# x + beta by accumulating DMA in every fourth group of a conditional residual adapter

## The chip, the cores and the metric

The kernel runs on one core of one Trainium2 chip. The metric is device time in microseconds, the median of the runs; the profile comes from one further execution. Engine names are those of the profile: PE is TensorE (PEld its weight loads), DVE is VectorE, ACT is ScalarE, POOL is GpSimd, SP is SyncE. A "q" behind an engine's name is its queue of instructions that aren't counted as work, DMA issues among them.

## The reference

There are 128 batches of 128 rows by 512 columns in float32, and 10 sets of weights. Batch b uses the set that `itok[b]` names.

```python
def ref(x, ids, W1, b1, W2, b2, gamma, beta):      # x: (128, 128, 512)
    h = relu(einsum('bsh,bha->bsa', x, W1[ids]) + b1[ids])      # A = 128
    z = x + einsum('bsa,bah->bsh', h, W2[ids]) + b2[ids]
    n = (z - mean(z)) * rsqrt(var(z) + 1e-5)
    return x + n * gamma[ids] + beta[ids]
```

## The kernel before

A batch is one tile of 128 rows by 512 columns. x is loaded in groups of four batches (1024 KB each) into four buffers by `load_x`, and the result is stored in pairs of batches (512 KB) by `store`; both are issued on SP. All ten rows of beta, gamma and b2 are first spread over the 128 partitions (`beta_b`, `gamma_b`, `b2_b`), and all of W1 and W2 stay in SBUF.

For one batch the work is this. PE transposes x in four pieces (`transpose_x`, L218), ACT copies the transpose out of PSUM (L222) and stages the batch's W1 (L209). PE multiplies (`down`, L241, 8 instructions), ACT applies the ReLU (L249), PE multiplies with W2 into a PSUM tile `py` (`up`, L258, 2 instructions), of which there are five. DVE adds the residual and sums the row (`residual`, L273), ACT sums squares (`square`, L288). DVE multiplies with gamma (`scale`, L322) and, once the reciprocal deviation of the pair is there (L305 to L317), multiplies and adds `o` in place (`finish`, L331). SP stores the pair.

The bias b2 enters in one of three ways. By default POOL makes r = x + b2 (`add_b2`, L228; four buffers), and the residual adds r in place of x. In some batches PE adds b2 by a small bfloat16 matmul ahead of the main one in `up` (`b2_by_matmul`, L257, 22 batches). In 13 others DVE adds it (`b2_by_vector`, L271). POOL also makes o = x + beta for every batch (`add_beta`, L235), into tiles of two batches, of which there are five.

The main loop is software-pipelined. Its iteration b has POOL make r of batch b + 2 and o of batch b; PE does `transpose_x` of b + 3, `down` of b + 2 and `up` of b + 1; DVE does the residual of b, `scale` of b - 2 and `finish` of b - 3. The store of a pair follows its second `finish`, in even iterations: iteration b stores the pair of batches b - 4 and b - 3. `keep` chains every instruction of an engine to the one before it, so that each engine's order is the order in which the program is written. In the kernel before, the stores are the exception: they are left to the scheduler.

For the last four batches the loop hands over to `tail`. There ACT normalizes batches 123, 124 and 125, and POOL multiplies two of them with gamma and adds o for all three (`by_pool`, L384 and L386, five instructions), while DVE finishes the rest. SP stores batches 122 to 127 one by one, in order (`store_last`, L389).

The first 16 batches use an early copy of W1 in another layout (`w1e`); the four loads of the later copy (`load_w1`, L111) are spread over the first iterations of the loop. A register that holds the batch's set number is loaded for four batches at a time on each engine that needs it (`lid`, L188).

Of the kernel before, what the change touches and what calls it, by code (L numbers as in the profile page):

```python
# [8 lines left out]
FP = mybir.dt.float32  # L9
# [3 lines left out]
ALU = mybir.AluOpType  # L13
ET = mybir.EngineType
PSUM = bass.MemoryType.PSUM

P = 128
G = 4
# [6 lines left out]
def cond_resid_kernel(ctx: ExitStack, tc: tile.TileContext, x, itok, W1, b1, W2, b2, gamma, beta, out):  # L25
# [8 lines left out]
    nc = tc.nc  # L34
    B, S, H = x.shape
    L, _, A = W1.shape
    KC = H // P
    NG = B // G
# [5 lines left out]
    def keep(ins):  # L44

        engine = ins.ins.engine
        if engine in last:
            tc.add_manual_dep(ins.ins, last[engine], behind, reason="kept order")
        last[engine] = ins.ins.name
        return ins  # L50
# [1 line left out]
    const = ctx.enter_context(tc.tile_pool(name="const", bufs=1))  # L52
    xp = ctx.enter_context(tc.tile_pool(name="xp", bufs=4))
    rp = ctx.enter_context(tc.tile_pool(name="rp", bufs=4))
    op = ctx.enter_context(tc.tile_pool(name="op", bufs=5))
    tp = ctx.enter_context(tc.tile_pool(name="tp", bufs=2))
    wp = ctx.enter_context(tc.tile_pool(name="wp", bufs=3))
    st = ctx.enter_context(tc.tile_pool(name="st", bufs=6))
# [5 lines left out]
    xs = {}  # L64

    def load_x(g):
        t = xp.tile([P, G, H], FP, tag="x", name=f"x_{g}")
        keep(nc.sync.dma_start(out=t, in_=x[g * G : (g + 1) * G].rearrange("b s h -> s b h")))
        xs[g] = t

    def xb(b):
        return xs[b // G][:, b % G, :]
# [27 lines left out]
    for l in range(0, L, 5):  # L100
        keep(
            nc.sync.dma_start(
                out=w1e[:, l : l + 5].rearrange("p l k a -> p l (k a)"),
                in_=W1[l : l + 5].rearrange("l (p k) a -> p l (k a)", k=KC),
# [4 lines left out]
    def load_w1(k):  # L109
        keep(  # L110
            nc.sync.dma_start(out=w1[:, :, k, :], in_=W1[:, k * P : (k + 1) * P, :].rearrange("l p a -> p l a"))  # L111
        )

    for l in range(0, L, 5):
        keep(
            nc.sync.dma_start(
                out=w2[:, l * H : (l + 5) * H].rearrange("p (l h) -> p l h", l=5),
                in_=W2[l : l + 5].rearrange("l a h -> a l h"),
# [48 lines left out]
    beta_b = const.tile([P, L * H], FP, name="beta_b")  # L167
# [14 lines left out]
    lids, xT, w1s, hT, rs, os, ys, ssqs, nmeans, rstds = {}, {}, {}, {}, {}, {}, {}, {}, {}, {}  # L182
    phs, pxs, sums = {}, {}, {}

    def lid(b, engine):
        g = b // G
        if (g, engine) not in lids:
            loads, vals = nc.values_load_multi_w_load_instructions(  # L188
                lang[0:1, g * G : (g + 1) * G],
                engines=[engine],  # L190
                min_val=0,
                max_val=L - 1,
                skip_runtime_bounds_check_because="clamped on the chip to 0..L-1 above",
            )
            for ins in loads:
                keep(ins)
            lids[g, engine] = vals
        return lids[g, engine][b % G]

    def b2_by_matmul(b):  # L200
        return b < 4 or (b % 4 == 1 and not b2_by_vector(b))

    def b2_by_vector(b):
        return b % 8 == 5 and 8 <= b < B - 16

    def stage_w1(b):
        w1s[b] = wp.tile([P, KC, A], FP, tag="w1s", name=f"w1s_{b}")
        src = (w1e if b < EARLY else w1).rearrange("p l k a -> p (l k a)")[:, bass.ds(lid(b, ET.Activation) * (KC * A), KC * A)]
        keep(nc.scalar.copy(w1s[b].rearrange("p k a -> p (k a)"), src))  # L209

    def transpose_x(b):
        pxs[b] = p_x.tile([P, KC, P], FP, tag="xT", name=f"pxT_{b}")
        for k in range(KC):
            if b < EARLY:
                cols = xb(b).rearrange("s (p k) -> s k p", k=KC)[:, k, :]
            else:
                cols = xb(b)[:, k * P : (k + 1) * P]
            keep(nc.tensor.transpose(pxs[b][:, k, :], cols, ident))  # L218

    def copy_xT(b):  # L220
        xT[b] = tp.tile([P, KC, P], FP, tag="xT", name=f"xT_{b}")
        keep(nc.scalar.copy(xT[b], pxs.pop(b)))  # L222

    def add_b2(b):
        if not b2_by_matmul(b) and not b2_by_vector(b):
            rs[b] = rp.tile([P, H], FP, tag="r", name=f"r_{b}")
            v = lid(b, ET.Pool)
            keep(nc.gpsimd.tensor_tensor(rs[b], xb(b), b2_b[:, bass.ds(v * H, H)], ALU.add))  # L228

    def add_beta(b):  # L230
        g, j = divmod(b, 2)
        if j == 0:
            os[g] = op.tile([P, 2, H], FP, tag="o", name=f"o_{g}")
        v = lid(b, ET.Pool)
        keep(nc.gpsimd.tensor_tensor(os[g][:, j, :], xb(b), beta_b[:, bass.ds(v * H, H)], ALU.add))  # L235

    def down(b):
        phs[b] = p_h.tile([P, P], FP, tag="h", name=f"ph_{b}")
        for k in range(KC):
            keep(  # L240
                nc.tensor.matmul(  # L241
                    phs[b], lhsT=w1s[b][:, k, :], rhs=xT[b][:, k, :], start=(k == 0), stop=(k == KC - 1)
                )
            )
        del xT[b], w1s[b]

    def relu(b):
        hT[b] = tp.tile([P, P], FP, tag="hT", name=f"hT_{b}", bufs=6)
        keep(nc.scalar.activation(hT[b], phs.pop(b), AF.Relu, bias=b1T[:, bass.ds(lid(b, ET.Activation), 1)]))  # L249

    def up(b):
        v = lid(b, ET.PE)
        ys[b] = p_y.tile([P, H], FP, tag="y", name=f"py_{b}")
        m = b2_by_matmul(b)
        if m:
            pick_b = pick[:, bass.ds(v + 2 * L, 1)].to_broadcast([96, P])
            keep(nc.tensor.matmul(ys[b], lhsT=pick_b, rhs=parts[:96, :], start=True, stop=False))  # L257
        keep(nc.tensor.matmul(ys[b], lhsT=hT[b], rhs=w2[:, bass.ds(v * H, H)], start=not m, stop=True))  # L258
        del hT[b]
# [5 lines left out]
    def residual(b):  # L265
        r = rs.pop(b) if b in rs else xb(b)
        if b % 2 == 0:
            sums[b // 2] = st.tile([P, 2], FP, tag="sum", name=f"sum_{b // 2}")
        if b2_by_vector(b):
            v = lid(b, ET.DVE)  # L270
            keep(nc.vector.tensor_tensor(ys[b], ys[b], b2_b[:, bass.ds(v * H, H)], ALU.add))  # L271
        keep(
            nc.vector.scalar_tensor_tensor(ys[b], ys[b], 1.0, r, ALU.mult, ALU.add, accum_out=col(sums, b))  # L273
        )
# [57 lines left out]
        )  # L332

    def store(g):
        nc.sync.dma_start(out=out[2 * g : 2 * g + 2].rearrange("b s h -> s b h"), in_=os.pop(g))
        del rstds[g]

    def on(b):
        return 0 <= b < B
# [151 lines left out]

    for i in range(3, B + U):
        b = i - U - 1
        if b > 0 and b % G == 0 and b // G + 3 < NG:
            load_x(b // G + 3)
        if i == 5:
            load_x(3)
        if i in (4, 6, 8, 10):
            load_w1((i - 4) // 2)
        if i == 4:  # L500
            up(2)
        if i == 5:
            up(3)
        if i > 3 and on(i):
            transpose_x(i)
        if b <= E:
            add_b2(b + 2)
            add_beta(b)
        if i > 4 and on(i - 1):
            down(i - 1)  # L510
        if i > 3 and on(i):
            copy_xT(i)
        if i > 4 and on(i + 1):
            stage_w1(i + 1)
        if i > 4 and on(i - 1):
            relu(i - 1)
        if i > 5 and on(i - U):
            up(i - U)


        g, half = divmod(b, 2)
        p = g - 1
        mine, old = 0 <= p < B // 2, 0 <= p - 1 < B // 2
        if b == E:
            add_b2(b + 3)
            add_beta(b + 1)
            add_b2(b + 4)
            for n in range(b + 2, B):
                add_beta(n)
        if b > E:  # L530
            tail(b)
        elif half == 0:
            if on(b):
                residual(b)
            if mine:
                rstd_1(p)
                scale(2 * p)
            if on(b):
                negative_mean(b)
            if mine:  # L540
                rstd_2(p)
            if old:
                finish(2 * p - 1)
                store(p - 1)
            if mine:
                rstd_3(p)
        else:
            if on(b):
                residual(b)
            if mine:  # L550
                rstd_4(p)
                scale(2 * p + 1)
            if on(b):
                negative_mean(b)
            if mine:
                finish(2 * p)
        if 0 <= b <= E:
            square(b)
            if half == 1:
                deviation(g)  # L560

        for n, engine in ((i + 3, ET.Activation), (i - U + 3, ET.PE), (b + 1, ET.DVE), (b + 5, ET.Pool)):
            if on(n):
                lid(n, engine)
# [37 lines left out]
```

## Time and profile before

| | us |
|---|---|
| median of 3 runs | 313.74 (313.61 to 314.29) |
| profiled execution | 313.83 |
| its span, first to last instruction | 312.1 |
| POOL, o = x + beta (L235), 128 of them | 161.6 busy, 1274 ns each |
| POOL, r = x + b2 (L228), 93 of them | 118.5 busy, 1274 ns each |
| PE, b2 by matmul (L257), 22 of them | 8.4 busy, 381 ns each |
| DVE, b2 (L271), 13 of them | 9.0 busy, 692 ns each |
| DMA, over the span | 75.49 MB, mean 242 GB/s |

In a row of groups, the busy time is the union of the instructions' times; an instruction's own duration can overlap its neighbours, so the distance from one start to the next is often shorter than the duration. "Idle before" is the time in which the engine stood still just ahead of such an instruction, with what ended it. The mean TensorE clock granted was 0.99. DMA issues list the time from issue to landing: 5.8 us at the median for a group of x, 3.9 for the store of a pair.

### The profile page before, as it was taken

Reading aid. Unit: us, or ns where it says so; the run is one execution under the profiler, and the core shown is the slowest. Engines: PE = TensorE matmul, PEld = TensorE weight load, DVE = VectorE, ACT = ScalarE, POOL = GpSimd, SP = SyncE. Lnnn points to the kernel's source line nnn. Section 1 sums busy time; section 2 is a strip of 40 time slices with the busy share of each in tenths; the row PEclk is TensorE's granted clock in tenths of the full one; section 3 lists DMA queues with packets and bytes.
Section 4 is the critical chain, followed back from the end, with each engine's and each line's share of the span. In section 5 each row is a group of like instructions: output and inputs, shape, how many; then the busy total and the mean of one; then the engine's idle time right before and its main releaser. Section 6 shows DMA issues by size and latency. Waiting matters only on the chain.

```text
span 312.1 us, 7096 instructions
## 1 busy us (share of the span) xinstructions
PE 300.5 (96%) x1869; PEld 223.8 (72%) x1869; DVE 297.3 (95%) x945; ACT 285.4 (91%) x724; POOL 280.1 (90%) x234
## 2 busy tenths in 40 slices
PE   8999999999999999999999999999999999999970
PEld 3567787777777767777777777777777777777740
DVE  6677999999999999999999999999999999999995
ACT  3878999999999999999999999999999999999982
POOL 1319978999999999999999999999999999999963
PEclk9999999999999999999999999999999999999995
DMA  6999998767776777667666567576666667633234
GB/s 209 387 387 352 326 339 275 238 229 226 236 250 225 255 265 269 242 231 270 257 227 226 210 238 253 213 272 269 232 232 198 232 247 239 244 134 138 88 149 168
DMA packets 42313, 75.49 MB, mean 242 GB/s; under 512 B 1785, under 2 KB 6916, under 8 KB 42274
## 3 DMA queue, kind: packets, MB, share of 16 engines
q1 hardware_dynamic: 42214, 75.00, 68.6%
q8 instruction: 15, 0.25, 0.3%
q14 instruction: 24, 0.20, 0.2%
q10 hardware_dynamic: 60, 0.05, 0.1%
HBM read 41.49 MB, written 33.55 MB: 240 GB/s over the span
## 4 chain that ended last, share of the span: by engine, by line
PE 91%; DVE 5%; ACT 1%; issue 1%; DVEq 1%; DMA 1%; ACTq 0%
PE ph L241 36%; PE py L258 34%; PE pxT L218 18%; PE py L257 1%; PE row L175 1%; DVE py L273 1%; DVE gamma_b L180 1%; DVE py L322 1%; DVE o L331 1%; DMA rows<-in_L_cond_b_dram 1%; ACT sq L366 0%; DVEq L597 0%; ACT n L382 0%; DVE left L156 0%; DVE left L154 0%
## 5 line engine op out<-in xcount | busy, mean ns | idle before, releaser
L235 POOL TENSOR_TENSOR o<-x,beta_b 128x512 f32<-128x512 f32 x128 | 161.6, 1274 | 12.8 <-ACT beta_b L178 9.2
L241 PE MATMUL ph<-xT,w1s 128*128 128x128 f32 x1024 | 135.6, 275 | 0.5 <-ACT w1s L209 0.5
L258 PE MATMUL py<-w,hT 128*128 x256 | 131.1, 594 | 0.0
L228 POOL TENSOR_TENSOR r<-x,b_b 128x512 f32<-128x512 f32 x93 | 118.5, 1274 | 11.5 <-DMA x<-in_x_dram 9.2
L241 PEld LDWEIGHTS ph<-xT,w1s 128*128 128x128 f32 x1024 | 124.7, 192 | 2.4 <-ACT w1s L209 1.0
L218 PEld LDWEIGHTS pxT<-ident,x 128*128 128x128 f32 x512 | 65.5, 148 | 64.9 <-issue 44.8
L322 DVE SCALAR_TENSOR_TENSOR py<-py,nmean,gamma_b 128x512 f32<-128x512 f32 x126 | 93.8, 745 | 0.2 <-issue 0.2
L331 DVE SCALAR_TENSOR_TENSOR o<-py,rstd,o 128x512 f32<-128x512 f32 x122 | 91.0, 746 | 0.0
L288 ACT ACTIVATE sq<-py,sum 128x512 f32<-128x512 f32 x124 | 85.3, 688 | 1.4 <-DVE py L273 1.3
L222 ACT COPY xT<-pxT 128x512 f32<-128x512 f32 x128 | 73.8, 577 | 9.8 <-PE pxT L218 6.3
L218 PE MATMUL pxT<-ident,x 128*128 128x128 f32 x512 | 77.4, 274 | 0.0
L209 ACT COPY w1s<-w 128x512 f32 x112 | 69.5, 621 | 0.0
L273 DVE SCALAR_TENSOR_TENSOR py<-py,r 128x512 f32<-128x512 f32 x93 | 64.6, 694 | 1.3 <-PE pxT L218 0.6
L249 ACT ACTIVATE hT<-ph,b1T 128x128 f32<-128x128 f32 x128 | 47.4, 370 | 1.0 <-PE ph L241 1.0
L258 PEld LDWEIGHTS py<-w,hT 128*128 128x128 f32 x256 | 40.6, 192 | 2.4 <-ACT hT L249 0.7
L273 DVE SCALAR_TENSOR_TENSOR py<-py,x 128x512 f32<-128x512 f32 x35 | 24.4, 697 | 1.6 <-ACT sq L288 0.6
L288 ACT ACTIVATION_READ_ACCUMULATOR sq<-py,sum 128x1 f32 x124 | 25.7, 208 | 0.0
L299 ACT ACTIVATE sd<-ssq,eps 128x2 f32<-128x2 f32 x62 | 18.3, 296 | 2.1
L279 DVE TENSOR_SCALAR nmean<-sum 128x1 f32<-128x1 f32 x128 | 19.5, 152 | 0.1
L305 DVE RECIPROCAL stat<-sd 128x2 f32<-128x2 f32 x62 | 13.0, 210 | 1.0 <-ACT sd L299 1.0
L273 DVE DVE_READ_ACCUMULATOR py<-py,r 128x1 f32 x93 | 13.4, 144 | 0.0
L317 DVE RECIPROCAL rstd<-stat 128x2 f32<-128x2 f32 x62 | 10.4, 168 | 0.0
(56 smaller groups left out, 120.6 us busy)
## 6 DMA issues: line engine op xcount, KB each, us to landing
out_dram<-o SPq DMA_DIRECT2D x61, 512.0 KB, 3.9
x<-in_x_dram SPq DMA_DIRECT2D x30, 1024.0 KB, 5.8
w1e<-in_L_cond_W_dram SPq DMA_DIRECT2D x2, 1280.0 KB, 8.7
w<-in_L_cond_W_dram SPq DMA_DIRECT2D x2, 1280.0 KB
w<-in_L_cond_W_dram SPq DMA_DIRECT2D x4, 640.0 KB, 15.2
x<-in_x_dram SPq DMA_DIRECT2D x4, 512.0 KB, 8.4
out_dram<-o SPq DMA_DIRECT2D x6, 256.0 KB, 2.0
rows<-in_L_cond_beta_dram ACTq DMA_DIRECT2D x1, 20.0 KB
```

What stands on the lines that cost most here:

```text
L209: keep(nc.scalar.copy(w1s[b].rearrange("p k a -> p (k a)"), src))
L218: keep(nc.tensor.transpose(pxs[b][:, k, :], cols, ident))
L222: keep(nc.scalar.copy(xT[b], pxs.pop(b)))
L228: keep(nc.gpsimd.tensor_tensor(rs[b], xb(b), b2_b[:, bass.ds(v * H, H)], ALU.add))
L235: keep(nc.gpsimd.tensor_tensor(os[g][:, j, :], xb(b), beta_b[:, bass.ds(v * H, H)], ALU.add))
L241: nc.tensor.matmul(phs[b], lhsT=w1s[b][:, k, :], rhs=xT[b][:, k, :], start=(k == 0), stop=(k == KC - 1))
L249: keep(nc.scalar.activation(hT[b], phs.pop(b), AF.Relu, bias=b1T[:, bass.ds(lid(b, ET.Activation), 1)]))
L258: keep(nc.tensor.matmul(ys[b], lhsT=hT[b], rhs=w2[:, bass.ds(v * H, H)], start=not m, stop=True))
L273: nc.vector.scalar_tensor_tensor(ys[b], ys[b], 1.0, r, ALU.mult, ALU.add, accum_out=col(sums, b))
L288: nc.scalar.activation(sq, ys[b], AF.Square, bias=col(sums, b), scale=-float(H), accum_out=col(ssqs, b))
L322: nc.vector.scalar_tensor_tensor(ys[b], ys[b], col(nmeans, b), gamma_b[:, bass.ds(v * H, H)], ALU.add, ALU.mult)
L331: nc.vector.scalar_tensor_tensor(o, ys.pop(b), rstds[g][:, j : j + 1], o, ALU.mult, ALU.add)
```

## The change

In every fourth group q of four batches (q = 3, 7, ..., 27), o = x + beta is no longer made by POOL. SP first copies the four batches' rows of `beta_b` into a tile `od` of four batches by four DMAs from SBUF to SBUF (`fill_beta`, in iteration 4q - 5). In iteration 4q - 2 POOL issues one DMA that adds the group's x onto that tile (`add_x`). `finish` and `store` then use the two halves of the tile as the `o` of the two pairs. There is one `od` tile, and four `o` tiles in place of five.

With that, b2 by matmul stays for batches 0 to 3 alone. DVE adds b2 in one batch of 16 from batch 21 to batch 101 in place of one of 8, and POOL makes r for all the others.

Groups of x from the fourth on are loaded two iterations later than before, and stores are kept in the program's order on SP.

```diff
-    op = ctx.enter_context(tc.tile_pool(name="op", bufs=5))
+    op = ctx.enter_context(tc.tile_pool(name="op", bufs=4))
+    od = ctx.enter_context(tc.tile_pool(name="od", bufs=1))
...
     def b2_by_matmul(b):
-        return b < 4 or (b % 4 == 1 and not b2_by_vector(b))
+        return b < 4
 
     def b2_by_vector(b):
-        return b % 8 == 5 and 8 <= b < B - 16
+        return b % 16 == 5 and 8 <= b < B - 16
...
+    def beta_by_dma(q):
+
+        return q % 4 == 3 and q < NG - 2
+
+    def fill_beta(q):
+
+        o = od.tile([P, G, H], FP, tag="od", name=f"od_{q}")
+        os[2 * q], os[2 * q + 1] = o[:, 0:2, :], o[:, 2:4, :]
+        for j in range(G):
+            v = lid(q * G + j, ET.SP)
+            keep(nc.sync.dma_start(out=o[:, j, :], in_=beta_b[:, bass.ds(v * H, H)]))
+        return o
+
+    def add_x(q, o):
+        keep(nc.gpsimd.dma_start(out=o, in_=xs[q], accum_op=ALU.add))
+
     def add_beta(b):
         g, j = divmod(b, 2)
+        if beta_by_dma(b // G):
+            return
...
     def store(g):
-        nc.sync.dma_start(out=out[2 * g : 2 * g + 2].rearrange("b s h -> s b h"), in_=os.pop(g))
+        keep(nc.sync.dma_start(out=out[2 * g : 2 * g + 2].rearrange("b s h -> s b h"), in_=os.pop(g)))
...
-        if b > 0 and b % G == 0 and b // G + 3 < NG:
+        if b > G and b % G == 2 and b // G + 3 < NG:
             load_x(b // G + 3)
...
+        q, at = divmod(b + 5, G)
+        if at == 0 and beta_by_dma(q):
+            filled = fill_beta(q)
+        q, at = divmod(b + 2, G)
+        if at == 0 and beta_by_dma(q):
+            add_x(q, filled)
         if b <= E:
             add_b2(b + 2)
             add_beta(b)
```

## The prediction

> **What bounds the kernel now.** I read the table of engines first, then the chain that ended last, the chain in order of time, the waits, and last the timeline of POOL beside that of DVE.
>
> ```profile
> PE 300.5 (96%) x1869; PEld 223.8 (72%) x1869; DVE 297.3 (95%) x945; ACT 285.4 (91%) x724; POOL 280.1 (90%) x234
> ...
> PE 91%; DVE 5%; ACT 1%; issue 1%; DVEq 1%; DMA 1%; ACTq 0%
> ```
>
> Four engines are above 90%, so shares alone decide nothing; the chain puts 91% on PE. Its pieces give PE's price for one batch:
>
> ```profile
> 179.74 0.89 PE ph L241 x8
> ...
> 181.93 0.89 PE ph L241 x8
> 182.82 0.22 PE py L257
> ...
> 184.34 0.89 PE ph L241 x8
> ```
>
> A batch without the L257 matmul takes 181.93 - 179.74 = 2.19 us, one with it 184.34 - 181.93 = 2.41. So the matmul costs 0.22 on the path, not the 381 ns that its row in the groups gives one, which overlaps its neighbours. DVE runs just under PE's pace: its residuals at 251.00, 253.05 and 255.24 are 2.12 apart on average. It lies one batch behind PE.
>
> POOL is the engine to watch. A POOL row says 1274 ns, but back to back one starts every 1.234 (252.11 to 261.97 holds eight). With 6 r and 8 o in eight batches it needs 14 x 1.234 = 17.3 of PE's 17.74, so it gains and runs ahead until it has no free r buffer:
>
> ```profile
> POOL n L384 <- ACT n L382: 2.3, 1, 2.3
> POOL r L228 <- DVE stat L305: 2.2, 6, 0.4
> ```
>
> ```profile
> 252.11 1.27 POOL L228 TENSOR_TENSOR r<-x,b_b 128x512 f32<-128x512 f32 x1
> 257.29 0.69 DVE L273 SCALAR_TENSOR_TENSOR py<-py,r 128x512 f32<-128x512 f32 x1
> ```
>
> In the timelines, the first line is r of batch 108, POOL's first work of iteration 106; the second is DVE's residual of batch 106. POOL's lead is 257.29 - 252.11 = 5.2 us there. The wait for n is what remains of it at the end: POOL is done with the last o at 298.7 and waits 2.3 for n of batch 123. After that five POOL instructions run without a gap to 307.41, and DVE ends at 308.74:
>
> ```profile
> 300.98 1.27 POOL L384 TENSOR_TENSOR n<-n,gamma_b 128x512 f32<-128x512 f32 x1 [2.28 <-ACT n L382]
> 304.93 2.48 POOL L386 TENSOR_TENSOR o<-n,o 128x512 f32<-128x512 f32 x2
> 307.33 1.41 DVE L393 SCALAR_TENSOR_TENSOR o<-py,rstd,o 128x512 f32<-128x512 f32 x2
> ```
>
> SP stores batch 125 (POOL's last) ahead of 126 and 127. POOL's last instruction can be late by about 0.6 (308.74 - 307.41, less two issues of 0.33 to 0.4) before it moves the end.
>
> **The Trainium skill.** "DMA: Bandwidth & Descriptors", SWDGE vs HWDGE vs iDMA: accumulation is only for DMAs issued from GpSimd, whose cores write the descriptors. Its section Latency and other measured facts puts the first byte at about 1 us because of that emission; the kernel before issues no DMA from POOL, so nothing here confirms it. "Collectives: The Full Stack", The bandwidth ceiling: the fold count and why AG ≠ RS ≠ AR: an adding DMA reads two sources per write and moves half as fast as a copy; not shown here either. "SBUF — State Buffer", SBUF: two separate sides: DVE holds GpSimd off the shared port in two-port modes or with two SBUF inputs. The trace shows no sign of such a lock: POOL's x instructions last 1256 to 1307 ns beside a DVE that is always busy. Its matrix operations mostly read one operand from PSUM, so I charge nothing for it.
>
> **Part by part.**
>
> *PE:* L257 goes from 22 to 4 (batches 0 to 3): 18 x 0.22 = 3.96 us less on the path.
>
> *DVE:* L271 goes from 13 to 6. Seven adds of about 0.7 lie beside PE; they only widen DVE's margin and buy nothing. ACT is unchanged.
>
> *POOL:* r rises from 93 to 118, o falls from 128 to 100: 25 - 28 = -3 instructions, 3.7 us less, and seven accumulating DMAs. In 16 batches POOL needs 27 x 1.234 = 33.3 plus one descriptor generation, c, where PE now needs 16 x 2.19 = 35.04: a margin of 1.7 - c. I take c = 1.0 from the skill's price. Below, 0.5: the mean cost can hardly be under the 0.3 to 0.9 of a register load on POOL's queue. Above, 2.5 (an estimate: the 1 us plus a doubled read side and a start that overlaps nothing).
>
> *SP and DMA:* 7 register loads (0.3 to 1.2 on other queues) and 28 fills of 256 KB on SP, in program order between stores. They cost nothing while SP waits for DVE, which its own waits show for most of the span. Transfers rise by 7 MB of fills and 7 MB of adds with twice the reads, over 75.5 MB now. The engines are at 0.64 to 0.72 between 60 and 260 us, so the mean fits; bunching is a rival below. Loading x two batches later leaves 7 iterations, 15 us, to its transpose against a median landing of 5.8: no cost. Kept stores move two w1 loads behind stores that wait for DVE at 32.6 and 36.6; from their bytes I put the last at 44 to 45, and ACT first needs it at 49.15: no cost.
>
> *The new wait:* POOL's adding DMA waits for the fills to land. Behind it on POOL stand r of the next batches, which DVE waits for. The fills stand on SP behind the store of iteration 4q-6, which waits for DVE, so POOL can no longer be ahead by more than the fills allow. For q = 27, in the clock of before: that store is issued at 251.05; add 0.37 for it, 0.7 for the register load, 4 x 0.5 for the fills: 254.1. Landing takes 2.0 at best (a 256 KB store in the tail), so 256.1; by bytes, 1.57 MB at 240 GB/s give 257.6 and more. I take 256.6. POOL may start r of 108 at 256.6 + 1.0 = 257.6, not at 252.1. The lead of 5.2 is gone.
>
> *What that costs at the end:* from there to n of 123 POOL has 20 r and 18 o: 38 x 1.234 = 46.9, so 304.5. PE's clock has by then gained 14 x 0.22 = 3.08 before 106, so 301.4; five instructions of the tail take 6.43: 307.8. SP then issues three stores, the last 0.8 later, and before there were 3.3 from DVE's end to the span's end: 307.8 + 0.8 + 3.3 = 311.9. PE alone would have given 312.1 - 3.96 = 308.1. **The tail on POOL thus takes back about 3.8 of the 3.96.**
>
> *What the first group costs:* for q = 3 the fills follow the w1 load on SP, at about 40 to 42, behind 3.4 MB queued since 32.6; at 330 to 390 GB/s they land near 46.5. POOL is there at 22.33 + 16 x 1.234 = 42.1. DVE wants residual 10 at 43.80 - 0.44 = 43.4, so the fill is 3.1 late. With c this is 4.1. The tightest need is r of 14, the fifth instruction after the add, done 6.2 later; DVE wants it four batches after residual 10, 8.8, so 2.6 can be borne. DVE waits 4.1 - 2.6 = 1.5. PE has some 0.8 to spare: the finish that ends at 202.16 frees the py that PE takes at 202.81, and the gap between `up` and residual adds a little. PE loses 0.7. Ends: 0 and 2.5.
>
> *Sum:* span 311.9 + 0.7 = 312.6. The profiled execution took 313.83 for a span of 312.1, 1.73 around it: 314.3. Its median of three is 0.09 lower, 313.74; I leave that aside.
>
> **Rivals.**
>
> *The gain stays (faster).* If c is at its low end and the fills land early, 254.1 + 2.0, the end moves by -0.5 - 0.5 - 0.7 from 314.3 to 312.6; if in addition POOL gets its r ahead of the wait, or the tail's store order matters less than I think, the end is PE's and the time 313.83 - 3.96 = 309.9. For it: PE is 91% of the chain. Against: the fills' place on SP. Between these, 311.
>
> *The adds land late (slower).* Finish of batch 4q needs the add. From its issue to that finish are five batches and 1.4, less c and the lateness: about 11 us in steady state, 8 in the first group. Alone it should take 5 to 7 (an x load's 5.8 at its median, with a read side doubled). Beside three stores and two loads in the same stretch it may take 12; from 11 on each extra us stops DVE, then PE, seven times. At 12: 7 x 1 more, 314.3 + 7 = about 321; the first group alone, 1 to 3 us.
>
> *Descriptors cost more than POOL's margin (slower).* From c = 1.7 on POOL falls behind by c - 1.7 in each period, and is the bound. It has 221 instructions from 22.33 on, 272.7 us, plus 7c and the first wait of 4.4, up to its tail's end: with c = 2.5, 316.9; plus 0.8, 3.3 and 1.73: 322.7.
>
> *The change does not do what it says:* the instruction order of the changed kernel has the 7 adds, 28 fills and 4 remaining L257; excluded.
>
> **How the numbers follow.** A measurement tells about 0.2%, 0.63 us, from no change. Tail on POOL takes the gain: 0.46, own range 312.6 to 316.5 (c 0.5 to 1.7, first group 0 to 2.5), of which faster 0.12, within 0.14, slower 0.20. Gain stays: 0.26, faster. Adds late: 0.16, slower. Descriptors: 0.12, slower. So faster 0.38, same 0.14, slower 0.48; the time is that of the likeliest case, 314.3, and 310.3 to 320 leaves out the full gain at its best and the worst of the last two.
>
> **What would show it.** L257 x4 and a batch of 2.19 everywhere. POOL's wait for a DMA before the adds, some 1 to 5 us, seven times at most. In the tail, no 2.3 us of POOL waiting for n, and POOL's last instruction behind DVE's, with the chain's end on POOL. If POOL still waits for n, the tail step is wrong. If DVE's finish waits for a DMA, the second rival holds; if DVE waits for r all along, the third.

## The result, and the profile after

The changed kernel takes **323.09 us** (median of four runs, 322.75 to 323.76), the kernel before on the same chip 313.72: ratio 1.0298, 95% interval 1.0276 to 1.0319. It is 3% slower, where 314.3 with a range up to 320 was forecast. The profiled execution took 323.76 for a span of 322.0, against 313.83 and 312.1 before.

The page of the changed kernel, its table of engines and the line of its chain that gives shares by engine:

```profile
PE 300.8 (93%) x1851; PEld 222.6 (69%) x1851; DVE 292.9 (91%) x938; ACT 285.7 (89%) x724; POOL 281.0 (87%) x238
...
PE 72%; POOL 9%; DVE 7%; issue 5%; DMA 2%; ACT 1%; POOLq 1%; SPq 1%; DVEq 0%; ACTq 0%
```

The matmul for b2 is left in four batches (its line, with lowest, median and highest duration in ns):

```profile
L276 PE MATMUL py<-parts,pick x4: 377/380/381, 21.6 to 25.3; 96*128 96x512 bf16 x4
```

PE had 91% of the chain and has 72%; POOL has come in with 9%. No engine's busy time rose by more than 0.9 us, so most of the 10 us are waiting. In these groups, those of the added DMA and of the r that POOL makes, the number ahead of the comma is the busy time, the one after it the mean duration in ns, and behind the bar's idle time stands what ended most of it:

```profile
L229 POOL TENSOR_TENSOR r<-x,b_b 128x512 f32<-128x512 f32 x118 | 165.2, 1472 | 8.9 <-DVE b_b L181 8.9
...
L245 POOL DMA_DIRECT2D od<-x x7 | 6.2, 891 | 17.1 <-DMA od<-beta_b 16.3
```

POOL stood still for 17.1 us ahead of seven adds, nearly all of it for the fills. Its waits and those of the engines behind it (us in total, times, longest):

```profile
POOL od L245 <- DMA od<-beta_b: 16.3, 5, 8.0
...
DVE py L292 <- POOL r L229: 6.7, 6, 4.4
...
PE py L277 <- DVE o L350: 3.2, 1, 3.2
```

The longest of each is one event, the first group: POOL waits 8.0, behind it DVE 4.4 for the r of batch 12, and behind that PE 3.2 for a free `py`. POOL's timeline around the first and the last add:

```profile
41.10 1.29 POOL L254 TENSOR_TENSOR o<-x,beta_b 128x512 f32<-128x512 f32 x1
50.38 1.01 POOL L245 DMA_DIRECT2D od<-x  x1 [7.99 <-DMA od<-beta_b]
51.13 1.55 POOL L229 TENSOR_TENSOR r<-x,b_b 128x512 f32<-128x512 f32 x1
...
263.68 0.87 POOL L245 DMA_DIRECT2D od<-x  x1 [2.66 <-DMA od<-beta_b]
264.29 1.57 POOL L229 TENSOR_TENSOR r<-x,b_b 128x512 f32<-128x512 f32 x1
```

The last line is r of batch 108, which began at 252.11 before. In the tail POOL no longer waits for n, and it ends behind DVE:

```profile
307.38 3.79 POOL L254 TENSOR_TENSOR o<-x,beta_b 128x512 f32<-128x512 f32 x3
311.04 1.35 POOL L403 TENSOR_TENSOR n<-n,gamma_b 128x512 f32<-128x512 f32 x1
...
315.03 2.48 POOL L405 TENSOR_TENSOR o<-n,o 128x512 f32<-128x512 f32 x2
```

```profile
312.36 1.41 DVE L412 SCALAR_TENSOR_TENSOR o<-py,rstd,o 128x512 f32<-128x512 f32 x2
```

POOL ends at 315.03 + 2.48 = 317.51, DVE at 313.77. From r of 108 to POOL's end there are 43 instructions in 317.51 - 264.29 = 53.2 us, 1.238 each, without a gap: **whatever delays the start at 264.29 comes out at the end, one for one.** Two questions follow: why this start is so late, and whether the tail is where it counts.

Why the first group is so late shows in the windows of the two kernels (stretch, its length, busy time of PE, PEld, DVE, ACT and POOL with counts, granted clock, DMA share, GB/s). Before:

```profile
32.00:36.00 4.00, 4.00 (x28) 3.30 (x27) 4.00 (x13) 3.81 (x11) 4.00 (x5) 1.00 1.09 353
```

After:

```profile
32.00:36.00 4.00, 4.00 (x27) 3.18 (x26) 4.00 (x15) 3.97 (x12) 4.00 (x4) 1.00 0.57 157
...
54.00:56.00 2.00, 1.02 (x2) 0.50 (x2) 1.85 (x9) 1.60 (x6) 2.00 (x2) 0.72 1.06 223
56.00:58.00 2.00, 2.00 (x8) 1.38 (x7) 1.71 (x4) 1.07 (x4) 2.00 (x3) 0.50 0.94 208
58.00:60.00 2.00, 2.00 (x13) 1.47 (x13) 1.88 (x8) 1.97 (x5) 2.00 (x3) 0.93 0.97 315
```

At 32 to 36 us the DMA engines moved 353 GB/s before and 157 after. The stores now stand in SP's order, SP waits at them for DVE, and the `load_w1` behind them are issued late. SP's timeline, before and then after, has the last two w1 loads at 29.41 to 34.35 and then at 33.67 and 37.91:

```profile
29.41 4.94 SPq L111 DMA_DIRECT2D w<-in_L_cond_W_dram  x2
```

```profile
33.24 0.39 SPq L354 DMA_DIRECT2D out_dram<-o  x1
33.67 0.47 SPq L112 DMA_DIRECT2D w<-in_L_cond_W_dram  x1
...
37.48 0.38 SPq L354 DMA_DIRECT2D out_dram<-o  x1
37.91 0.90 SPq L112 DMA_DIRECT2D w<-in_L_cond_W_dram  x1
40.08 2.88 SPq L241 DMA_DIRECT2D od<-beta_b  x4
```

They now stand right ahead of the fills, which SP issues from 40.08 to 42.96 and which have landed at 49.8, as the chain in order of time shows:

```profile
42.41 7.39 DMA od<-beta_b
```

The last three lines of the windows show what came on top: after PE's wait the granted clock fell to 0.72, 0.50 and 0.93, which is 2 x (0.28 + 0.50 + 0.07) = 1.7 us of PE time. PE's timeline after:

```profile
49.44 1.02 PE L277 MATMUL py<-w,hT 128*128 x2
...
54.98 2.08 PE L277 MATMUL py<-w,hT 128*128 x2 [3.19 <-DVE o L350]
```

The second line, `up` of batch 14, began at 51.51 before. PE's offset (start of `up` of a batch, less the same in the kernel before) goes from +0.12 at batch 13 to +3.47 at 14 and +5.18 at 15.

### The profile page after: what moved, and what is told of

It reads as the page before. It is cut to its first block, busy times and chain, and to the rows that moved or that the text cites. A ratio compares the mean times of both kernels' runs of the same rounds, so it can differ in the third digit from the quotient of the medians.

```text
span 322.0 us, 7085 instructions
## 1 busy us (share of the span) xinstructions
PE 300.8 (93%) x1851; PEld 222.6 (69%) x1851; DVE 292.9 (91%) x938; ACT 285.7 (89%) x724; POOL 281.0 (87%) x238
## 4 chain that ended last, share of the span: by engine, by line
PE 72%; POOL 9%; DVE 7%; issue 5%; DMA 2%; ACT 1%; POOLq 1%; SPq 1%; DVEq 0%; ACTq 0%
PE py L277 27%; PE ph L260 27%; PE pxT L219 14%; POOL r L229 4%; POOL o L254 3%; DMA od<-beta_b 2%; PE idle L474 2%; DVE py L292 2%; DVE py L341 2%; PE row L176 1%; DVE gamma_b L181 1%; DVE od L350 1%; DVE o L350 1%; POOL o L405 1%; POOL n L403 1%
## 5 line engine op out<-in xcount | busy, mean ns | idle before, releaser
L229 POOL TENSOR_TENSOR r<-x,b_b 128x512 f32<-128x512 f32 x118 | 165.2, 1472 | 8.9 <-DVE b_b L181 8.9
L254 POOL TENSOR_TENSOR o<-x,beta_b 128x512 f32<-128x512 f32 x100 | 142.4, 1443 | 9.7 <-ACT beta_b L179 9.7
L277 PE MATMUL py<-w,hT 128*128 x256 | 132.9, 601 | 3.8 <-DVE o L350 3.2
L292 DVE SCALAR_TENSOR_TENSOR py<-py,r 128x512 f32<-128x512 f32 x118 | 81.7, 692 | 9.9 <-POOL r L229 6.7
L350 DVE SCALAR_TENSOR_TENSOR o<-py,rstd,o 128x512 f32<-128x512 f32 x94 | 69.9, 744 | 0.0
L277 PEld LDWEIGHTS py<-w,hT 128*128 128x128 f32 x256 | 39.3, 193 | 6.9 <-DVE o L350 4.2
L350 DVE SCALAR_TENSOR_TENSOR od<-py,rstd,od 128x512 f32<-128x512 f32 x28 | 20.8, 744 | 0.8 <-DVE nmean L298 0.6
L245 POOL DMA_DIRECT2D od<-x x7 | 6.2, 891 | 17.1 <-DMA od<-beta_b 16.3
L292 DVE DVE_READ_ACCUMULATOR py<-py,r 128x1 f32 x118 | 16.8, 142 | 0.0
```

The costliest lines, as they stand in the source:

```text
L350: nc.vector.scalar_tensor_tensor(o, ys.pop(b), rstds[g][:, j : j + 1], o, ALU.mult, ALU.add)
```

## The experiments

All were timed beside the kernel before, which had medians of 313.7 to 313.9 on each chip. Theory 1 says that the loss is the sum of two things, the late fills of the first group and POOL's unbroken tail. Theory 2 says that the adds' DMA traffic slows every group alike.

**The first group without a DMA add.** Six groups are left, from q = 7 on.

```diff
-        return q % 4 == 3 and q < NG - 2
+        return q % 4 == 3 and 3 < q < NG - 2
```

> The first group by DMA (q = 3) is left to POOL as in the kernel before; the six later groups stay. Theory 1 (POOL's own sum sets the end: instructions at 1.23 us plus its waits for fills): the wait of 8.0 us goes, four more o cost 4.9, one descriptor generation of 0.6 less; PE's loss of some 5 us at batches 12 to 15 goes too, so POOL is early at the next fill and is held there until the fill lands, as far behind DVE as before (about 2.4 us). Time about 318, DVE's wait for r of batch 12 gone. Theory 2 (the adds' DMA traffic is the cost, alike in each group): one seventh of the 9.4 us comes back, about 321.7.

Measured: 318.13 us (316.18 to 318.63), ratio 1.0127 (1.0097 to 1.0157). One group out of seven gives back 323.09 - 318.13 = 5.0 us, what PE's offset had said (5.18 - 0.12 = 5.06): theory 1. That the two agree so well is in part luck, for the four runs lie 2.5 us apart. PE's offset has no jump, is -0.07 at batches 12 to 16 and -1.37 at the end. The last rows of its timelines of POOL and of DVE:

```profile
309.63 2.48 POOL L405 TENSOR_TENSOR o<-n,o 128x512 f32<-128x512 f32 x2
```

```profile
306.95 1.41 DVE L412 SCALAR_TENSOR_TENSOR o<-py,rstd,o 128x512 f32<-128x512 f32 x2
```

POOL still ends 3.8 behind DVE (312.1 against 308.4). The second half of theory 1 is not touched by this.

**The tail's b2 on PE.** Batches 113, 117, 121 and 125 go back to `b2_by_matmul`; POOL has four r less after 264.29.

```diff
-        return b < 4
+        return b < 4 or (b % 4 == 1 and b >= B - 16)
```

> b2 of batches 113, 117, 121 and 125 is by matmul again, as before; all else as changed. Theory 1: four instructions fewer in POOL's unbroken run to the end, 4.9 us; PE gets 0.9 more, off the path; time about 318.2 and POOL's last instruction near DVE's. Theory 2 (traffic; PE's and DVE's delay sets the end): up by 0 to 0.9, 323 to 324.

Measured: 318.15 us (316.25 to 319.61), ratio 1.0136 (1.0098 to 1.0173). Four instructions of 1.234 are 4.94, and the median fell by 323.09 - 318.15 = 4.9. The last rows of POOL and of DVE:

```profile
309.02 2.48 POOL L405 TENSOR_TENSOR o<-n,o 128x512 f32<-128x512 f32 x2
```

```profile
311.42 1.41 DVE L412 SCALAR_TENSOR_TENSOR o<-py,rstd,o 128x512 f32<-128x512 f32 x2
```

Now POOL is done at 311.5, ahead of DVE's 312.8. In the two profiled executions POOL's end moved by 6.0 (317.5 to 311.5): 4.9 are the four instructions, and the rest is that r of 108 began 1.2 earlier, at 263.12. So the tail was POOL's, and with four instructions less it is DVE's. As DVE sets the end now, it is in part luck that the median fell by just the four instructions.

The first group of this kernel is that of the changed kernel, but in this execution PE lost 6.9 us in it and not 5.1: its offset goes from +0.13 to +7.05. It waited 3.65 for a free `py`, and the clock stayed low for longer:

```profile
54.00:56.00 2.00, 0.55 (x1) 0.50 (x2) 1.85 (x7) 2.00 (x5) 2.00 (x3) 0.70 1.01 216
56.00:58.00 2.00, 2.00 (x6) 0.92 (x5) 1.76 (x6) 1.09 (x4) 2.00 (x3) 0.50 0.98 217
58.00:60.00 2.00, 2.00 (x11) 2.00 (x10) 1.95 (x7) 1.10 (x2) 2.00 (x3) 0.50 0.94 293
60.00:62.00 2.00, 2.00 (x7) 0.86 (x6) 0.45 (x3) 1.04 (x3) 2.00 (x3) 0.59 0.90 314
```

That is 2 x (0.30 + 0.50 + 0.50 + 0.41) = 3.4 us of PE time, twice the 1.7 of the changed kernel's trace. The 5 us of the first group are thus the price in one execution.

**Both.** The two edits together.

> No DMA add in the first group and b2 of 113, 117, 121 and 125 by matmul. Theory 1: both gains add up, since both are taken out of one sum: 318.1 - 4.9, then PE's and DVE's own end takes over near 313; 313 to 314. Rival (each run lost to a different limit): 316 or more.

Measured: **312.62 us** (20 runs, 311.48 to 314.53), ratio 0.9960 (0.9948 to 0.9972), a little under the 313 to 314 that was expected: the gains add, and the kernel is 0.4% faster than before. POOL ends at 305.5 and DVE last, at 306.8; PE's offset begins at +0.82 and ends at -1.98: 2.8 of the 3.08 that its 14 matmuls less are worth. The two terms, and no others of their size, make the loss.

**The w1 loads ahead of the stores.** The changed kernel with all seven groups, but `load_w1` in iterations 0 to 3 in place of 1, 3, 5 and 7 (`i` in the code is the iteration plus 3).

```diff
-        if i in (4, 6, 8, 10):
-            load_w1((i - 4) // 2)
+        if i in (3, 4, 5, 6):
+            load_w1(i - 3)
```

> The changed kernel with the four w1 loads in iterations 0 to 3 in place of 1, 3, 5 and 7, so that none stands behind a kept store. Theory 1 with the idle DMA as the reason for the first fill's lateness: the DMA rate of 32 to 36 us rises from 157 GB/s to over 300, the first fill lands some 3 us earlier, DVE's wait for r of batch 12 falls from 4.4 to 1 to 2, and 2 to 4 us come back: 319 to 321. Rival (the fill itself is slow beside other transfers): the wait stays over 3.5, time within 1 of 323.

Measured: 317.75 us (317.07 to 318.63), ratio 1.0117 (1.0102 to 1.0132): 5.3 back, more than was expected. The windows:

```profile
32.00:36.00 4.00, 4.00 (x28) 3.30 (x27) 4.00 (x15) 3.97 (x11) 4.00 (x4) 1.00 1.14 322
...
52.00:54.00 2.00, 1.13 (x4) 0.61 (x5) 1.85 (x9) 1.60 (x6) 2.00 (x3) 1.00 1.02 217
54.00:56.00 2.00, 2.00 (x14) 1.57 (x13) 1.70 (x4) 1.97 (x6) 2.00 (x3) 1.00 0.96 218
```

And POOL's first add and DVE's wait behind it, from their timelines:

```profile
48.26 1.01 POOL L245 DMA_DIRECT2D od<-x  x1 [4.11 <-DMA od<-beta_b]
```

```profile
50.61 0.70 DVE L292 SCALAR_TENSOR_TENSOR py<-py,r 128x512 f32<-128x512 f32 x1 [2.66 <-POOL r L229]
```

The DMA engines are full at 32 to 36 us again, PE waits 1.4 and keeps its clock of 1.00. PE's offset goes from -0.23 to +1.87, 2.1 instead of 5.06. POOL's wait for the fills is 4.11 and was 7.99, but that says too much: 1.7 of the difference it now waits elsewhere, for an `o` tile to be stored. The add starts 2.1 earlier, because the fills land 2.1 earlier, at 40.71 + 6.97 = 47.68 and not at 49.80:

```profile
40.71 6.97 DMA od<-beta_b
```

The w1 loads behind the stores are thus shown to make the first fill 2.1 us late, and these 2.1 cost PE some 3. The 4.11 that remain are a wait that the first group has with the w1 loads out of the way as well. In the two traces r of batch 108 begins at 264.29 and 259.15, 5.1 apart: 0.3 arose before the first group, 3.0 in it, 0.8 between it and the residual of 106, and 1.1 at the last fill.

**Fills two iterations earlier.** The same, tried from the other side.

```diff
-        q, at = divmod(b + 5, G)
+        q, at = divmod(b + 7, G)
         if at == 0 and beta_by_dma(q):
             filled = fill_beta(q)
```

> The fills are issued in iteration 4q-7 in place of 4q-5, the adds stay. Theory 1: the fills land about 4.4 us earlier, POOL's later waits (8.3 us in all) go nearly to zero and that of the first group falls from 8.0 to about 3.6; DVE waits for r of batch 12 about 0.5 in place of 4.4. Time about 313 to 316. Theory 2: the traffic is the same, time within 1.5 of 323. A third possibility: SP now waits for the od tile's store to land and holds loads and stores behind it; then new waits for x or for o show.

Measured: a median of 321.7 where 313 to 316 was expected, but four runs from 316.01 to 323.55, so no ratio is given. The trace is of a run of 321.1; whether the run of 316.01 had the same waits isn't known. POOL's waits for fills are gone, as intended. In their place the fills stand ahead of the last w1 load on SP, which is issued at 39.34. The waits in 40 to 62 us:

```profile
DVE py L292 <- PE py L277: 5.5, 1, 5.5
ACT w1s L210 <- DMA w<-in_L_cond_W_dram: 4.3, 1, 4.3
...
PE ph L260 <- ACT hT L268: 3.7, 1, 3.7
```

ACT waits for W1, PE for ACT, and the clock falls to 0.50 again: PE's offset rises from -0.36 to +5.11. Neither theory foresaw this. In this execution the stretch before 50 us had no room for fills and w1 loads at once, and the edit only chose which of the two is late. The waits for o that were named as a third possibility show too: POOL waits 6.8 us in six places for an `o` tile to be stored. And the end is still POOL's, at 314.8, where DVE is done at 311.45. Early fills and early w1 loads together, with all seven groups, were not tried.

**The DMA adds without the r's.** `b2_by_matmul` and `b2_by_vector` as in the kernel before; POOL has 25 r less than the changed kernel.

> The DMA half alone: b2 is divided as in the kernel before (22 by matmul, 13 by DVE, 93 by POOL). POOL has 25 fewer instructions than the changed kernel, PE has 18 matmuls more. Theory 1: the first group's fill still lands near 50 and still stops DVE by 4 to 5 us; from the last fill on POOL has 38 instructions to its end in place of 43 and no longer sets it; DVE's end does: about 319 to 321. Theory 2: 313.7 plus the traffic's 9 to 12: 323 to 326.

Measured: 319.37 us (318.31 to 320.38), ratio 1.0178 (1.0153 to 1.0202). Its waits:

```profile
POOL od L245 <- DMA od<-beta_b: 35.1, 7, 9.9
...
DVE py L292 <- POOL r L229: 4.1, 1, 4.1
```

POOL waits 35 us for fills, five a group, and DVE feels one of them, the first: a lead that POOL can win back costs nothing. PE's offset goes from +0.08 to +4.89 in the first group and to +6.08 at the end. Six further groups of fills and adds cost PE 1.2 us together in this execution, 0.2 each, where the first cost 4.8; theory 2, which has them alike, falls. What six groups cost is scattered, though. Up to batch 106 the kernel without the first group and the one with both edits are the same program; the 12 matmuls saved between the two places are worth 2.64 to PE, and in their traces it gained 0.6 and 2.35. So the six groups took 2.0 in one execution and 0.3 in the other.

**Order alone.** The kernel before with kept stores and x loaded two iterations later; then the same with `load_w1` first.

> The kernel before with only the order changed: stores kept in program order on SP and x loaded two iterations later. No add by DMA, b2 divided as before. Theory 1 (POOL's sum and the first group's late fill are the cost): no more than 0.5 from 313.7. Rival (the order on SP itself costs, since two w1 loads stand behind stores that wait for DVE and the DMA engines idle from 32 to 36 us): ACT waits for w1 near 49 us and the time is 315 to 318.

> The order alone (kept stores, x two iterations later), with the w1 loads in iterations 0 to 3. If the two w1 loads behind stores are why the order alone is 0.6 slower, the time is 313.9, as before; if it is the stores' or the x loads' place in the steady part, it stays near 314.5.

Measured: 314.46 us (12 runs, ratio 1.0018, 1.0010 to 1.0027) and 314.35 (17 runs, ratio 1.0023, 1.0013 to 1.0034). The DMA engines have the same gap at 32 to 36 us in the first of them (207 GB/s), but with no fills behind it PE and ACT show no wait that the kernel before hasn't. The order by itself costs some 0.6 us, and the w1 loads are not its reason. About 0.5 of it lies after DVE's last instruction (3.85 us to the span's end, 3.36 before); its cause stays open.

**Can more be had?** Three kernels on top of the last edits: both edits and early fills; both edits and w1 loads first; the tail's edit and w1 loads first, with all seven groups.

> As the run with two edits, and the fills in iteration 4q-7. No w1 load is near the fills now (the first is that of q = 7). Theory 1: POOL no longer waits for fills (5.6 us in the run without the first group) and is off the path; PE's 18 - 4 matmuls less, 3.1 us, show but for what the late adds cost DVE: 310.6 to 312.5, faster than the kernel before. Theory 2 (the traffic of six groups costs 1.3 us each): no faster than 314.

> The run with two edits (no DMA add in the first group, b2 of 113, 117, 121 and 125 by matmul), and the w1 loads in iterations 0 to 3. If the idle DMA of 32 to 36 us is what the kept order costs (0.6 in the run of the order alone), about 312.0; if it has no effect without a fill behind it, 312.6. Either is faster than before.

> All seven groups by DMA, the w1 loads first, and b2 of 113, 117, 121 and 125 by matmul. Theory 1: the last two terms come out of one sum: 317.75 - 4.9 = 312.9 as long as POOL sets the end; DVE's and PE's end, 1.6 to 2 us late from the first group, is near 313 too: 312.9 to 314. Rival (the first group can't be had for less than leaving it out): 315 or more.

Measured: 312.65 us (6 runs, ratio 0.9964, 0.9952 to 0.9976), 313.44 (22 runs, 0.9995, 0.9977 to 1.0012) and 313.88 (20 runs, 1.0011, 0.9997 to 1.0025). With early fills POOL waits for n again (0.36), as in the kernel before, so POOL is off the path; still the time is just over the 310.6 to 312.5 that was expected, and nothing is gained over the two edits. PE's offset in that trace goes from -0.11 at the place of the first group to -1.6 at its end; the 12 matmuls saved in between are worth 2.64, so some 1.1 is lost in the stretch with the adds. Early w1 loads bring nothing once the first group is gone, where 312.0 to 312.6 was expected: their ratio is 0.0035 above that of the two edits alone, and why it is worse isn't settled. With all seven groups, they and the tail's edit give the same time as before, which is the sum of the terms (317.75 - 4.9 = 312.9) to within 1. The best are the two kernels at 312.6.

## Why the prediction was wrong, step by step

**Right.** L257 (L276 after) is there four times, and a batch costs PE 2.19. POOL's spacing is 1.23, its tail has no wait for n, and its last instruction lies behind DVE's. The step that decided, "the fills' place on SP" ending POOL's lead and the tail on POOL taking the gain, is what happened. From r of 108 on the sum held: 43 x 1.234 = 53.1 against 53.2, and 0.8 + 3.3 = 4.1 against 322.0 - 317.5 = 4.5.

**Wrong: the start of that tail.** The step that failed is the forecast of when the fills land and POOL may go on. It was too early for the first group (46.5 forecast, 49.8 measured), so that PE's loss there was put at 0.7 and was 5.06, and too early for the last (5.6 us after the store forecast, 8.0 measured). The prediction has r of 108 at 257.6 - 3.08 + 0.7 = 255.2; it was 264.29, 9.1 late, and the span of 322.0 is 9.4 above the 312.6 forecast. The terms:

| term | predicted, us | measured, us | error, us |
|---|---|---|---|
| PE's offset before the first group (up to batch 10) | -0.44 | +0.12 | 0.56 |
| first group: loss of PE | 0.70 | 5.06 | 4.36 |
| 12 matmuls less (batches 17 to 105), up to the residual of 106 | -2.64 | -0.54 | 2.10 |
| r of 108 after the residual of 106 | 0.31 | 2.36 | 2.05 |

The sum is 9.1. The residual of 106, which the third line takes from the 257.29 of before, is DVE's in its timeline after:

```profile
261.93 0.70 DVE L292 SCALAR_TENSOR_TENSOR py<-py,r 128x512 f32<-128x512 f32 x1
```

*Before the first group.* The two matmuls less gave what was forecast: from batch 0 to 10 the offset falls by 0.44. But this execution began 0.57 behind the kernel before. In the traces of the experiments, whose programs are the same up to there, batch 0 begins between -0.02 and +0.82: this is the scatter of executions.

*First group.* Two premises failed. "Behind 3.4 MB queued since 32.6 at 330 to 390 GB/s" took the DMA engines for busy; they moved 157 GB/s until 36, because SP stood at the kept stores. The prediction had moved two w1 loads behind those stores and asked only whether W1 would be late. It was not ("no cost" held), but the same bytes now lay ahead of the fills, which landed at 49.8 and not at 46.5. Of these 3.3 the early w1 loads took back 2.1; the other 1.2 stay open. And the borrowing, "so 2.6 can be borne" and "PE has some 0.8 to spare", was computed against a wait of 4.1: at 8.0 all of it is used up, DVE stands at the r of 12 already, and not only at that of 14, and PE stands still for 3.2. The 1.7 for the lost clock was in no term.

*Steady state.* For q = 27 the add started 8.0 after the store's issue (255.69 to 263.68), not 5.6 (251.05 to 256.6). The issues took 3.5 in place of 3.1, and the landing after the last issue 4.5 in place of 2.5. Beside it the DMA engines are at a share of 0.91 in 100 to 140 us, after 0.71 before; that this is why is argued, not tested. The error is in "I take 256.6", the low side of an estimate whose other end ("257.6 and more") was written down.

*Later groups.* Taken as free. They took 2.1 of the 2.64 up to the residual of 106, 1.7 of it on PE. As the other traces show 0.3 to 2.0 on PE for six groups, much of this term can be the scatter of executions, and where it arises stays open.

*Descriptor generation.* c was too high. From the start of the add to the next r it is 264.29 - 263.68 = 0.61 in the last group and 0.75 in the first, not 1.0. The Trainium skill ("DMA: Bandwidth & Descriptors", Latency and other measured facts) puts the first byte at about 1 us; that is the latency of a transfer, and POOL was held for less.

**The rivals.** "The gain stays" fails: the end is POOL's. "Descriptors" fails, since 0.61 is under the margin of 1.7, though its 322.7 lies nearest to the result, by luck, and its sum has the right form: POOL's serial time is 221 x 1.232 = 272.3 and 7 x 0.61 = 4.3, from 22.6 on, and with the 17.1 of standing still it ends at 316.3, 1.2 short of the measured end. The waits for fills make the end, not the descriptors. "Adds late" named the right threshold, but nothing near its 7: the adds landed after 9.6 to 12.0 us (median 11.0), around its 11, and in four of the seven groups DVE began the group's first `finish` 0.09 us after the landing. So it waited for the add there, though the profile names another instruction of DVE; but these waits are 0.02 to 0.62, some 0.75 us together. The longest is that of batch 92, whose add landed at 238.74:

```profile
238.83 0.75 DVE L350 SCALAR_TENSOR_TENSOR od<-py,rstd,od 128x512 f32<-128x512 f32 x1 [0.62 <-DVE nmean L298]
```

## What to carry to other kernels

An engine that runs ahead of the others keeps its lead only as long as nothing it does has to wait for a queue that is tied to their pace; a fill on SP behind a store that waits for DVE ends it. Price the first such group by itself: at start-up, loads moved behind stores leave the DMA engines empty and then crowd out whatever is issued next, even if they come in time for their own use. And as single executions lost 0.3 to 2.0 us in the same six groups, trace a term more than once before trusting a difference of that size. Then count the helper's unbroken chain from its last wait to the end: any instruction in it costs its full time, so give that stretch back to the engine that has room.

## What the runs showed of the hardware

- A PE wait of some 3 us cost more than itself. After waits of 3.2, 3.65, 3.7 and 2.9 us (the changed kernel, the tail's b2 on PE, early fills, adds without r's) the granted clock fell to 0.50 in at least one stretch of 2 us; after 1.4 and 1.2 (w1 loads first, without and with the tail's edit) it stayed at 1.00. The slow clock took 1.7 us of PE time in the first of these and 3.4 in the second. The Trainium skill ("TensorE: Matmul & The Clock Gate", Part 1) says that the clock is halved after an idle window of about 3.4 us. The two longer waits agree; 2.9 and 3.2 were enough here as well.
- An adding DMA of 1 MB occupied POOL for 0.6 to 0.75 us, though its row shows 0.87 to 1.01 in the same trace.
- POOL's x instructions showed longer durations after an adding DMA (1.29 us before the first one, 1.55 behind it; mean 1472 ns for r, 1274 in the kernel before), while their spacing stayed at 1.23. The duration is not the price. The traffic as such is not the reason: with early fills the DMA engines are at a share of 0.93 in 100 to 140 us, and r has a mean of 1289 ns. What is stays open.
- The kernels with adds varied more from run to run: 311.5 to 314.5 for the best one, 313.6 to 314.9 for the kernel before beside it.
